# Two graph layers on listed neighbours: node rows two blocks ahead of the lists, and both weight folds moved to a later stage

## The chip, the cores and the metric

The kernel runs on one core of a Trainium2 chip. The metric is the device time of one execution in microseconds: 727.7 us, the median of three runs (726.72 to 728.53). One of these executions was also profiled; its span is 725.5 us, at a mean granted TensorE clock of 0.977. Engines are named as in the profile: PE is TensorE's matmul, PEld its weight load, DVE VectorE, ACT ScalarE, POOL GpSimd, SP the queue of SyncE.

## What is computed

`x` is 4096 x 512, `adj` a 4096 x 4096 matrix of int32 with about four ones in a row. Layer 0 is graph attention with eight heads, layer 1 a mean over neighbours with two linear maps and a third on their concatenation:

```python
# layer 0: W (8, 512, 64), a (8, 128)
Wh = einsum('nf,hfo->hno', x, W)
f1 = einsum('hno,ho->hn', Wh, a[:, :64]);  f2 = einsum('hno,ho->hn', Wh, a[:, 64:])
e  = leaky_relu(f1[:, :, None] + f2[:, None, :], 0.2)
attn = softmax(where(adj > 0, e, -9e15))
x  = layernorm(x + concat_heads(attn @ Wh))
# layer 1
deg = sum(adj > 0)
agg = (adj > 0) @ x / max(deg, 1)
y = concat(x @ W_self + b_self, agg @ W_nb + b_nb) @ W_comb + b_comb
x = layernorm(x + relu(y))
```

## The kernel before

The rows are taken in 32 blocks of 128. The adjacency is never used as a matrix: it is turned into a list of neighbours for each row, and the two layers gather their neighbours' rows by index. (A dense path, `dense_layers`, stands behind a flag and does not run on these inputs.) There are three stages, and each engine executes its own queue in the order of the program text (`manual_schedule`), so the text fixes what waits behind what.

**Lists and node rows (to about 245 us).** For each block `b`, `load_adj` brings two halves of 1 MB of `adj` into four buffers (`at`). `mask_adj` (ScalarE, L367) turns a half into bf16 (`ab`, three buffers) and so frees the list buffer. `fold_adj` (TensorE, L379) adds the eight segments of each row into one number per column, from which `decode` can read column and segment: a first matmul puts the column numbers into a PSUM bank (`cols`, weighted by `two`), two more add the weighted bits. `max_keys` (VectorE, L393) takes the largest eight of each quarter. Every four blocks, `decode` turns these keys into lists in five parts, one in each following iteration: keys apart; the top 16; degrees and the first three indices; the offsets of what is left over and the rows `sts` that assign it; and the "shared" slots (`es`, two a block) that take those neighbours beyond three. In the same iteration the node block's row is computed: `transposed` (L304, its copy L306), then `node_half` twice (L312), eight matmuls each, against `w_sb`, which holds W and, in eight columns on either side, W times the two halves of `a`. The result (`row`) is stored to `t0` in DRAM by ScalarE's queue.

Ahead of this stage stands a prologue: w0 is loaded, the extra columns of `w_sb` are computed in 32 operations of VectorE (L722, L727), and `fold_weights` computes `m2 = W_nb @ W_comb` (lower half) with its bias (L251 to L285). The list loads are issued behind the 2 MB of these weights.

**Attention (about 245 to 510 us).** `gather` (GpSimd, L508) fetches for each block three plus two rows of `t0` by index, five indirect transfers a block, into five buffers (GA). A loop over `i` from -2 to 33 runs the steps of different blocks against each other: `a_weights`, `a_exp`, `a_sum` for block i+2; `a_reach`, `a_normed`, `a_weigh`, `a_shared` (L595) for i+1; `a_moments` (L611), `root`, `norm` for i; and for i-1 `a_z` (L632), which multiplies the new row by `m2` and stores it to `t1`. In the first turns the last list parts and `m1 = W_self @ W_comb` (upper half) are worked in: `some(lists)`, `some([folds])`.

**Second layer (510 to 725 us).** Gathers from `t1`, five a block again; `g_self` (L656) with `m1`, `g_shared` (L663), adds, the norm, and the store. A gather buffer is free again when `g_shared` and the adds of the block five earlier are through.

PSUM has the banks `key` (1), `nm` (2), `pw` (2), `tp` (1) and `sm` (2). Small results go round in the two `sm` banks.

Of the kernel before, what the change touches and what calls it, by code (L numbers as in the profile page):

```python
# [22 lines left out]

# [16 lines left out]
P = 128  # L40
# [44 lines left out]
def listed_layers(  # L85
# [32 lines left out]
    EX = KX + 2 + 1 + H  # L118
# [67 lines left out]
    )  # L186
    two = const.tile([P, 32], BF16, name="two")
# [20 lines left out]
    es = const.tile([P, NB, KH, EX], F32, name="es")  # L208
    idx = const.tile([P, NB, KS], U32, name="idx")
# [4 lines left out]
    m1 = const.tile([P, FB, HD], F32, name="m1")  # L214
    brow = const.tile([P, HD], F32, name="brow")
    bc = const.tile([1, HD], F32, name="bc")
# [13 lines left out]
    def load_fold(k, w, fp):  # L230
        wr = fp.tile([P, FB, HD], F32, name="wr")
        (nc.sync, nc.scalar)[k].dma_start(wr, w.rearrange("(c p) o -> p c o", p=P))
        wc = fp.tile([P, FB, HD], F32, name="wc")
        (nc.sync, nc.scalar)[k].dma_start(
            wc, w_comb[k * HD : (k + 1) * HD, :].rearrange("(c p) o -> p c o", p=P)
        )
        return wr, wc
# [6 lines left out]
    def fold_weights(loaded, m, wp, tag="pw", last=None):  # L244

        wr, wc = loaded

        def turned(c):
            tp = ps.tile([P, FB, P], F32, name="nm", bufs=2)
            for d in range(FB):  # L250
                nc.tensor.transpose(tp[:, d, :], wr[:, c, ts(d, P)], ident)  # L251
            t = wp.tile([P, FB, P], F32, name="xT", bufs=2)
            nc.scalar.copy(t, tp)
            return t

        wT = turned(0)
        for c in range(FB):
            nxt = turned(c + 1) if c + 1 < FB else last and last()
            t = "pw" if c + 1 < FB else tag
            mp = ps.tile([P, HD], F32, name=t, bufs=2 if t == "pw" else 1)  # L260
            for d in range(FB):
                nc.tensor.matmul(  # L262
                    mp, lhsT=wT[:, d, :], rhs=wc[:, d, :], start=(d == 0), stop=(d == FB - 1)
                )
                if t != "pw" and d == FB // 2 - 1:
                    yield
            nc.scalar.copy(m[:, c, :], mp)
            wT = nxt
            yield

    def fold_bias(loaded, brw, to, tag):
# [5 lines left out]
        bp = ps.tile([1, HD], F32, name=tag, bufs=1)  # L277
        for d in range(FB):
# [4 lines left out]
            if d == FB // 2 - 1:  # L283
                yield
        nc.vector.tensor_add(brow[0:1, :], bp, to)  # L285
# [9 lines left out]
    def load_x(b, xacc):  # L295
        if b < NB:
            nc.sync.dma_start(xs[:, b, :], x[ts(b, P), :])
            nc.gpsimd.tensor_tensor(xacc, xacc, xs[:, b, :], OP.add)  # L298
# [19 lines left out]
    def node_rest(b, row):  # L318
# [3 lines left out]
        )  # L322

    def mean_row(w_sb, xacc, wp):
# [7 lines left out]
        nc.vector.tensor_copy(xm, pm)  # L332
        mr = wp.tile([P, HD], F32, name="y", bufs=2)
        mf = small.tile([1, H], F32, name="mf", bufs=1)
        for k in range(2):
# [9 lines left out]
            if k == 0:  # L345
                nc.vector.tensor_copy(mf, pq[:, 0:H])
        nc.scalar.dma_start(t0[1:2, 0:H], mf)
        nc.scalar.dma_start(t0[1:2, H:TW], mr[0:1, :])

# [3 lines left out]
    def load_adj(b, ap):  # L353

        if b < NB:
            for h in range(NH):
                at = loads[b, h] = ap.tile([P, NG // NH, SC], I32, name="at", bufs=4)
                r = b * P + h * (P // NH)
                nc.sync.dma_start(
                    at, adj[r : r + P // NH, :].rearrange("(j r) (s c) -> (r s) j c", r=RG, s=SEG)  # L360
                )

    def mask_adj(b, h, ap):
        if b == NB:
            return
# [5 lines left out]
    def fold_adj(b, dp):  # L371
# [3 lines left out]
        )  # L375
        ab = [masks.pop((b, h)) for h in range(NH)]
        for k in range(3):
            for t in range(P // 32):
# [4 lines left out]
                    start=(k == 0), stop=(k == 2), tile_position=(0, 32 * t),  # L383
                )
# [10 lines left out]
    def decode(b0, dp, wp):  # L395
# [48 lines left out]
        if b0 + G == NB:  # L444
            yield
        for b in range(b0, b0 + G):
            lt = wp.tile([P, KH * P], F32, name="st", bufs=2)
            nc.vector.tensor_scalar(lt, iota[:, 0 : KH * P], end[:, b : b + 1], None, OP.is_lt)
            if b0 + G < NB:
                st = wp.tile([P, KH * P], F32, name="own", bufs=4)  # L450
            else:
                if b % 2 == 0:
                    rows = wp.tile([P, FW], F32, name="row", bufs=2)
                st = rows[:, b % 2 * KH * P : (b % 2 + 1) * KH * P]
            nc.vector.scalar_tensor_tensor(
                st, iota[:, 0 : KH * P], lst[:, b, KL : KL + 1], lt, OP.is_ge, OP.mult
            )
            sts.append(st)
        yield
        pe = ps.tile([P, G, KH, EX], F32, name="sm", bufs=2)  # L460
# [6 lines left out]
        if b0 + G == NB:  # L467
            yield
        nc.vector.tensor_copy(es[:, bs], pe)
        if b0 + G == NB:  # L470
            yield
# [33 lines left out]
    def gather(table, b, gp):  # L505
        g = gp.tile([P, KS, TW], F32, name="g")
# [22 lines left out]
    def a_weights(b, wp):  # L529
        gw = G0[b][:, :, 0:H]  # L530
        e = E[b] = wp.tile([P, KS, H], F32, name="e", bufs=3)
        nc.vector.tensor_tensor(
            e[:, 0:K0, :], gw[:, 0:K0, :],
            lst[:, b, KL + 3 :].unsqueeze(1).to_broadcast([P, K0, H]), OP.add,
        )
        nc.vector.tensor_add(e[:, K0:KS, :], gw[:, K0:KS, :], es[:, b, :, KX + 3 :])
# [48 lines left out]
    def a_x(b):  # L585

        NM[b] = ps.tile([P, HD], F32, name="nm", bufs=2)
        if b < 2:
            nc.tensor.matmul(NM[b], lhsT=ident, rhs=xs[:, b, :], start=True, stop=False)
        else:  # L590
            nc.scalar.copy(NM[b], xs[:, b, :])

    def a_shared(b):
        for k in range(KH):
            nc.tensor.matmul(  # L595
                NM[b], lhsT=OWN[b][:, k, :], rhs=G0[b][:, K0 + k, H:TW],
                start=False, stop=(k == KH - 1), skip_group_check=b > 1,
# [88 lines left out]
    wp = ctx.enter_context(tc.tile_pool(name="work", bufs=1))  # L686
    dp = ctx.enter_context(tc.tile_pool(name="decode", bufs=1, side="right"))
    ap_cm = tc.tile_pool(name="lists", bufs=1, side="right")
    ap = ap_cm.__enter__()
    xa = ctx.enter_context(tc.tile_pool(name="xa", bufs=1))  # L690
    xacc = xa.tile([P, FIN], F32, name="xacc")
    nc.gpsimd.memset(xacc, 0.0)
    w_sb = xa.tile([P, FB, FW], F32, name="w_sb")
    with tc.tile_pool(name="wa", bufs=1) as wa:
        arow = wa.tile([1, H, 2, D], F32, name="arow")
        nc.scalar.dma_start(arow, a0.rearrange("h (k d) -> h k d", k=2).unsqueeze(0))
        for h in range(H):
            nc.sync.dma_start(
                w_sb[:, :, H + h * D : H + (h + 1) * D], w0[h].rearrange("(c p) o -> p c o", p=P)
            )  # L700
        loaded = load_fold(1, w_nb, wa)
        brw = load_bias(1)
        nc.scalar.dma_start(bc, b_comb.rearrange("(a o) -> a o", a=1))
        load_x(0, xacc)
        load_x(1, xacc)
        load_adj(0, ap)
        load_x(2, xacc)
        load_x(3, xacc)
        load_adj(1, ap)
        for b in range(4, XL):  # L710
            load_x(b, xacc)
        pads(wp)
        av = []
        for k in range(2):
            av.append(ps.tile([P, H, D], F32, name=("key", "sm")[k], bufs=(1, 2)[k]))
            nc.tensor.matmul(av[k], lhsT=oner, rhs=arow[:, :, 1 - k, :], start=True, stop=True)
        for a in range(2):
            for k in range(2):
                for c in range(FB):
                    pr = wa.tile([P, H // 2, D], F32, name="pr", bufs=2)  # L720
                    cs = slice(H + a * HH, H + (a + 1) * HH)
                    nc.vector.tensor_mul(  # L722
                        pr, w_sb[:, c, cs].rearrange("p (h d) -> p h d", d=D),
                        av[k][:, a * 4 : a * 4 + 4, :],
                    )
                    f = k * TW + a * 4
                    nc.vector.tensor_reduce(w_sb[:, c, f : f + 4], pr, AX.X, OP.add)  # L727
        last = {}

        def first():  # L730
            last["xT"] = transposed(0, wp)

        pieces = fold_weights(loaded, m2, wp, last=first)
        for c in range(FB):
            next(pieces)
            if 1 <= c <= 2:
                mask_adj(0, c - 1, ap)
        next(pieces, None)
        for _ in fold_bias(loaded, brw, bc, "key"):
            pass  # L740
    fp = ctx.enter_context(tc.tile_pool(name="fold", bufs=1))


    xT = last["xT"]
    row, lists = None, []
    for b in range(NB):
        load_x(b + XL, xacc)
        load_adj(b + 2, ap)
        if b == NB - 2:
            loaded = load_fold(0, w_self, fp)  # L750
            brw = load_bias(0)
        if b < NB - 1:
            for p in lists:
                next(p, None)
        mask_adj(b + 1, 0, ap)
        nxt = transposed(b + 1, wp) if b + 1 < NB else None
        if b > 0:
# [534 lines left out]
```

## Time and profile before

| stretch, us | what runs | transfers, GB/s | of note |
|---|---|---|---|
| 0 to 18.1 | loads, columns of `w_sb`, start of the fold | 278 | VectorE busy 10.06 us |
| 18.1 to 36.3 | fold of `m2`, first masks | 358 | TensorE busy 17.61 us |
| 36.3 to 54.4 | first blocks | 279 | |
| 72.5 to 229 | lists and node rows | 392 | VectorE 117.09 of 156.5 us |
| 245 to 290 | last list parts, fold of `m1`, first gathers | 196 | mean TensorE clock 0.85 |
| 290 to 500 | attention | 199 | TensorE 207.42, VectorE 192.81 of 210 us |
| 512 to 705 | second layer | 249 | GpSimd 145.87 of 193 us |

The table is read by stretches, since the stages have different limits and the shares of the whole span (PE 90%, DVE 68%, ACT 59%, POOL 48%) mix them. GpSimd's busy time counts 0.95 us of each gather; the next one starts 1.25 us after it, so a stretch with 78% is one in which GpSimd never rests. Some times that are used below: the masks of the last list start at 232.97 and 236.01; the first gather of attention starts at 246.14; the first `a_z` at 287.5, the second at 295.67; the first gather of the second layer at 509.78.

### The profile page before, as it was taken

What the parts mean: (1) busy time and instruction counts of PE and PEld (TensorE: products, weight loads), DVE (VectorE), ACT (ScalarE), POOL (GpSimd) and SP (SyncE); (2) the same over time, 40 slices, a digit from 0 to 9 for tenths busy, and PEclk for the clock granted to TensorE, in tenths of its full rate; (3) what the DMA queues carried; (4) which work ended last, traced back from release to release, by engine and by line L of the source; (5) the groups of instructions that cost most, each with busy time, mean ns of one, the idle gap of its engine ahead of it and who ended that gap; (6) DMA issues with size and microseconds to landing.
All of it is one profiled execution on the core that took longest, in us unless ns stands there. A gap on an engine that the chain in (4) does not pass through costs nothing.

```text
span 725.5 us, 9190 instructions
## 1 busy us (share of the span) xinstructions
PE 650.8 (90%) x2654; PEld 358.1 (49%) x2654; DVE 493.5 (68%) x1474; ACT 430.3 (59%) x883; POOL 348.5 (48%) x368
## 2 busy tenths in 40 slices
PE   4998888887899899999999999998999999999972
PEld 1465656655666654555555555554444444443320
DVE  5236777877877676899999999994255555554552
ACT  1566667666677123565766657665466666666653
POOL 3421122122100377566666666500677777777771
PEclk9999999999999889999999999999999999999995
DMA  9979999999999477677787887711588888878882
GB/s 278 358 279 394 393 393 392 392 393 392 392 393 389 163 211 211 185 230 230 226 234 225 230 230 229 227 41 39 173 257 250 252 252 255 251 249 249 250 256 101
DMA packets 84248, 191.29 MB, mean 264 GB/s; under 512 B 12496, under 2 KB 12504, under 8 KB 84190
## 3 DMA queue, kind: packets, MB, share of 16 engines
q0 software_dynamic: 25600, 84.56, 40.6%
q1 hardware_dynamic: 52896, 95.43, 35.7%
q10 hardware_dynamic: 5694, 10.64, 4.0%
q8 instruction: 23, 0.38, 0.2%
q14 instruction: 35, 0.29, 0.1%
HBM read 165.29 MB, written 25.31 MB: 263 GB/s over the span
## 4 chain that ended last, share of the span: by engine, by line
PE 50%; DMA 19%; POOL 10%; issue 9%; DVE 6%; ACT 5%; ACTq 0%; POOLq 0%; SPq 0%; DVEq 0%
PE pw L632 16%; POOL g L508 10%; DMA at<-in_adj_dram 9%; PE nm L595 8%; PE pw L312 7%; DMA g<-t,idx 6%; ACT xT L306 3%; PE pw L262 3%; PE tp L304 3%; DMA t<-row 2%; PE pw L663 2%; PE sm L546 2%; PE sm L463 1%; DMA w_sb<-in_L_gnn_W_dram 1%; PE nm L656 1%
## 5 line engine op out<-in xcount | busy, mean ns | idle before, releaser
L508 POOL DMA_INDIRECT g<-t,idx x320 | 303.3, 948 | 211.8 <-issue 120.2
L367 ACT ACTIVATE ab<-at 128x2048 bf16<-128x2048 int32 x64 | 122.2, 1910 | 62.9 <-DMA at<-in_adj_dram 56.1
L312 PE MATMUL pw<-w_sb,xT 128*128 128x264 f32 x512 | 127.6, 393 | 0.0
L632 PE MATMUL pw<-m,xT 128*128 128x512 f32 x256 | 118.4, 605 | 3.4 <-ACT xT L306 1.7
L298 POOL TENSOR_TENSOR xacc<-xacc,xs 128x512 f32<-128x512 f32 x32 | 41.3, 1292 | 148.7 <-DMA xs<-in_x_dram 148.2
L312 PEld LDWEIGHTS pw<-w_sb,xT 128*128 128x128 f32 x512 | 92.2, 190 | 26.1 <-issue 3.8
L306 ACT COPY xT<-tp 128x512 f32<-128x512 f32 x80 | 46.2, 578 | 72.1 <-PE tp L304 71.9
L580 DVE TENSOR_TENSOR g<-g,key 128x1024 f32<-128x1024 f32 x64 | 77.8, 1216 | 1.1
L632 PEld LDWEIGHTS pw<-m,xT 128*128 128x128 f32 x256 | 46.0, 189 | 56.8 <-issue 45.9
L304 PE MATMUL tp<-ident,xs 128*128 128x128 f32 x320 | 49.5, 277 | 26.3 <-ACT xT L306 25.3
L304 PEld LDWEIGHTS tp<-ident,xs 128*128 128x128 f32 x320 | 37.9, 141 | 61.0 <-ACT xT L306 32.2
L595 PE MATMUL nm<-g,own 128*128 128x512 f32 x128 | 62.7, 612 | 0.0
L656 PE MATMUL nm<-m,xT 128*128 128x512 f32 x128 | 57.7, 593 | 1.3 <-ACT xT L306 1.3
L656 PE MATMUL pw<-m,xT 128*128 128x512 f32 x128 | 57.6, 592 | 0.0
L316 DVE COPY row<-pw 128x264 f32<-128x264 f32 x64 | 27.3, 427 | 41.7 <-DMA t<-row 17.5
L642 ACT COPY sm<-g 128x512 f32<-128x512 f32 x32 | 18.9, 590 | 50.8 <-DMA g<-t,idx 47.8
L648 DVE TENSOR_TENSOR y<-sm,g 128x512 f32<-128x512 f32 x32 | 22.1, 691 | 30.8 <-DMA g<-t,idx 30.5
L663 PE MATMUL pw<-g,own 128*128 128x512 f32 x64 | 34.2, 651 | 9.0 <-DMA g<-t,idx 6.0
L663 PE MATMUL nm<-g,own 128*128 128x512 f32 x64 | 34.1, 641 | 8.4 <-DMA g<-t,idx 4.1
L656 PEld LDWEIGHTS nm<-m,xT 128*128 128x128 f32 x128 | 23.1, 190 | 24.5 <-issue 23.0
L646 DVE TENSOR_TENSOR sm<-sm,g 128x512 f32<-128x512 f32 x32 | 22.3, 697 | 18.6 <-DMA g<-t,idx 17.8
L670 DVE SCALAR_TENSOR_TENSOR sm<-y,lst,nm 128x512 f32<-128x512 f32 x16 | 12.1, 755 | 33.5 <-PE nm L663 33.5
(176 smaller groups left out, 1006.0 us busy)
## 6 DMA issues: line engine op xcount, KB each, us to landing
at<-in_adj_dram SPq DMA_DIRECT2D x64, 1024.0 KB, 10.8
t<-row ACTq DMA_DIRECT2D x32, 260.0 KB, 5.7
xs<-in_x_dram SPq DMA_DIRECT2D x32, 256.0 KB, 6.0
t<-row SPq DMA_DIRECT2D x32, 256.0 KB, 3.4
out_dram<-row SPq DMA_DIRECT2D x32, 256.0 KB, 3.7
g<-t,idx POOLq DMA_INDIRECT x320, 4.1
w_sb<-in_L_gnn_W_dram SPq DMA_DIRECT2D x8, 128.0 KB, 7.6
wr<-in_L_gnn_W_nb_dram ACTq DMA_DIRECT2D x1, 1024.0 KB, 7.2
```

The lines of the kernel that those rows point to most:

```text
L298: nc.gpsimd.tensor_tensor(xacc, xacc, xs[:, b, :], OP.add)
L304: nc.tensor.transpose(tp[:, c, :], xs[:, b, ts(c, P)], ident)
L306: nc.scalar.copy(t, tp)
L312: nc.tensor.matmul(pw, lhsT=xT[:, c, :], rhs=w_sb[:, c, k * HW : (k + 1) * HW], start=(c == 0), stop=(c == FB - 1),)
L316: nc.vector.tensor_copy(row[:, k * HW : (k + 1) * HW], pw)
L367: nc.scalar.activation(ab, loads.pop((b, h)), AF.Relu, accum_out=asum[:, b, h : h + 1])
L508: nc.gpsimd.indirect_dma_start(out=g[:, k, 0 : table.shape[1]], out_offset=None, in_=table[:, :], in_offset=bass.IndirectOffsetOnAxis(ap=i ...
L580: nc.vector.tensor_tensor(gv if to is None else to.rearrange("p (k h d) -> p k h d", k=1, h=H), gv, E[b][:, sl].unsqueeze(3).to_broadcast( ...
L595: nc.tensor.matmul(NM[b], lhsT=OWN[b][:, k, :], rhs=G0[b][:, K0 + k, H:TW], start=False, stop=(k == KH - 1), skip_group_check=b > 1,)
L632: nc.tensor.matmul(pz, lhsT=xT[:, c, :], rhs=m2[:, c, :], start=(c == 0), stop=(c == FB - 1))
L656: nc.tensor.matmul(NM[b], lhsT=xT[:, c, :], rhs=m1[:, c, :], start=False, stop=False, skip_group_check=True,)
L663: nc.tensor.matmul(NM[b], lhsT=OWN[b][:, k, :], rhs=g[:, K0 + k, 0:HD], start=False, stop=(k == KH - 1), skip_group_check=True,)
```

## The change

Several edits, meant to shorten the way to the first list load and to the first gather:

- **w0 first.** The prologue no longer loads or folds `w_nb`. w0, x's first block (on ScalarE's queue) and the lists come first. The extra columns of `w_sb` are computed in six operations of VectorE and two multiplications of GpSimd on tiles of 128 x 1024.
- **Node rows two blocks ahead.** The index `w` of the node block runs ahead of the list block `b`: in iterations 6 and 12 two node blocks are computed (`AHEAD`). So the loop over lists ends at block 29 with all rows in `t0`, and the lists 30 and 31 are folded while the first gathers run.
- **ScalarE writes the columns into the fold's bank.** `key_bank` copies the column numbers (`colf`) into the PSUM bank, and `fold_adj` leaves out its first matmul, save in blocks 0, 1 and 3, where each of the three banks is first used. The order of ScalarE in an iteration is now: `xT`, `key_bank`, store, both masks.
- **Last lists in the turn.** The parts of the last decode are spread over the first turns of attention (i = -2 to 0).
- **z's weights last.** `w_nb` and `w_comb` are loaded behind the last list, and `m2` is folded in chunks, one ahead of the attention loop and one in each of i = -2, -1, 0; its bias follows at i = 1. `m1` and its bias are folded between attention and the second layer. There is one buffer for `wT` where there were two.
- Small ones: `f1` of the neighbours' receivers is laid out once in `f1s` (GpSimd and VectorE), so `a_weights` needs one addition and not two; `a_x` is ScalarE's copy for all blocks.

```diff
     def decode(b0, dp, place):
...
+        nc.vector.tensor_copy(es[:, bs], pe[:, :, :, 0:EX])
+        nc.vector.tensor_copy(f1s[:, bs, K0:KS, :], pe[:, :, :, EX:])
...
+    def key_bank(b):
+        key = keys[b] = ps.tile([P, SC], F32, name=("key", "nm")[b % 2], bufs=(1, 2)[b % 2])
+        if b not in FIRST:
+            nc.scalar.copy(key, colf)
...
     def fold_adj(b, dp):
-        for k in range(3):
+        for k in range(0 if b in FIRST else 1, 3):
...
+    av = fp.tile([P, FB, HD], F32, name="wr")
+    nc.scalar.dma_start(av[0:1, 0:2]..., a0...)
+    for h in range(H):
+        nc.sync.dma_start(w_sb[:, :, H + h * D : H + (h + 1) * D], w0[h]...)
+    load_x(0, nc.scalar)
+    load_adj(0, ap)
+    load_x(1)
+    load_x(2)
+    load_adj(1, ap)
+    for b in range(3, XL):
+        load_x(b)
...
+    for a in range(2):
+        times(nc.gpsimd, a, pr1[a], av[:, 0])
+    times(nc.vector, 0, pr2, pa[1])
+    summed(0, 0, pr2)
+    times(nc.vector, 1, pr2, pa[1])
+    summed(1, 0, pr2)
+    summed(0, 1, pr1[0])
+    summed(1, 1, pr1[1])
...
+    for b in range(LB):
+        for k in range(1 + (b in AHEAD)):
+            load_x(w + k + XL)
+            sum_x(w + k + XL, xacc)
+        load_adj(b + 2, ap)
...
+        if b == LB - 1:
+            loaded = load_fold(1, w_nb, fp)
+        some(lists)
+        nxt = transposed(w + 1, wp) if w + 1 < NB else None
+        key_bank(b + 1)
+        if w > 0:
+            store(w - 1, row)
+        for h in range(NH):
+            mask_adj(b + 1, h, ap)
+        row = node_block(w, xT, b)
+        w, xT = w + 1, nxt
+        if b in AHEAD:
+            nxt = transposed(w + 1, wp)
+            store(w - 1, row)
+            row = node_block(w, xT)
+            w, xT = w + 1, nxt
...
+    mask_adj(NB - 1, 0, ap)
+    store(NB - 1, row)
...
+    for b in range(2):
+        G0[b] = gather(t0, b, gps)
+    m2s = chain(fold_weights(loaded, m2, fp, ("pw", "pw", "tp", "tp")), fold_bias(loaded, brw))
+    fold_adj(LB, dp)
+    max_keys(LB)
+    mask_adj(NB - 1, 1, ap)
+    key_bank(NB - 1)
     some(lists)
+    some(lists)
+    fold_adj(NB - 1, dp)
+    max_keys(NB - 1)
...
+    some(lists)
+    lists = [decode(NB - G, dp, on_rows)]
+    some(lists)
     a_owners(0, wp)
     a_owned(0, wp)
+    for k in range(3):
+        next(m2s)
     some(lists)
...
     for i in range(-2, NB + 2):
...
+        if i < 1:
+            for k in range(3):
+                next(m2s)
+        if i < 1:
             some(lists)
         if i == 1:
-            spread_bias()
+            for k in range(2):
+                next(m2s)
...
+            loaded = load_fold(0, w_self, fp)
+            brw = load_bias(0)
+    m1s = chain(fold_weights(loaded, m1, fp, ("key", "tp", "key", "tp")), fold_bias(loaded, brw))
+    for _ in m1s:
+        pass
+    spread_bias()
+    G1 = {b: gather(t1, b, gps) for b in range(GA - 1)}
```

## The prediction

> **What bounds the kernel now.** I read the forty-slice part of the page first, then stretches of busy time, then the chain of waits, then single engines in order of time. The kernel has three stages with different limits: lists and node rows up to 245 us, attention to 510, the second layer to 725.
>
> The stretches (columns: stretch, length, busy PE, PEld, DVE, ACT, POOL, clock, DMA share, GB/s) give the first limit:
>
> ```profile
> 0.00:40.00 40.00, 28.57 (x77) 13.13 (x77) 16.08 (x51) 12.69 (x19) 15.63 (x26) 1.00 0.97 319
> 40.00:46.00 6.00, 6.00 (x47) 3.83 (x45) 2.42 (x9) 4.36 (x5) 0.81 (x1) 1.00 0.35 119
> 46.00:229.00 183.00, 156.66 (x1010) 111.40 (x1007) 132.67 (x527) 123.12 (x138) 28.67 (x22) 1.00 1.05 391
> ```
>
> From 46 us on the transfers run at 391 GB/s and no engine is full: the adjacency stream is the limit. Before that it is starved. From 40 to 46 us it drops to 119 GB/s, because ScalarE's masks (L367), which free the list buffers, wait behind the weight fold of the prologue.
>
> In the attention stage the chain of waits (start, length, what) has a fixed rhythm:
>
> ```profile
> 400.32 3.70 PE pw L632 x8
> 404.02 0.34 PE sm L546 x4
> 404.37 1.82 PE nm L595 x4
> 406.19 0.45 PE tp L304 x4
> 406.64 0.02 issue
> 406.66 0.59 ACT xT L306
> 407.25 0.04 issue
> 407.30 3.70 PE pw L632 x8
> ```
>
> One block is 6.98 us: TensorE, plus the one copy it waits for. VectorE is on none of it. In the second layer GpSimd's gathers (L508) start every 1.25 us without a gap from 509.78 to the last at 708.81: 160 gathers, 200 us, and a tail of 15.7 us. There GpSimd's issue is the limit.
>
> At the seam between lists and attention two fold chunks of eight matmuls stand in TensorE's order of time:
>
> ```profile
> 249.66 4.97 PE L262 MATMUL pw<-wc,xT 128*128 128x512 f32 x8
> 255.12 3.60 PE L262 MATMUL pw<-wc,xT 128*128 128x512 f32 x8
> ```
>
> The same work takes 4.97 and 3.60 us; the mean clock in 247 to 249 us is 0.50. The slow one follows a wait.
>
> **What the Trainium skill says.** "TensorE: Matmul & The Clock Gate", What's actually happening: the array runs at half clock after about 3.4 us of idling, at full clock after about as much sustained work. The trace agrees on the halves (4.97 against 3.60); an idle time of 2.11 us ahead of 244.54 was already followed by slow matmuls. "DMA: Bandwidth & Descriptors", Issuing engines are not separate DMA queues: a load moved to another issuing engine saves only its issue time. So x's first block on ScalarE's queue counts as nothing here; no row isolates it. "GPSIMD Engine Reference", Elementwise: a two-input operation takes GpSimd about twice VectorE's time. Here 128x512 takes 1.29 us (L298) against 0.70 (L605).
>
> **Part 1, the stream: minus 9.9 us.** The stretch up to 54 us, summed in steps of 2 us, misses 4.8 MB against 393 GB/s, or 12.3 us. The start (first 4 us: 3 and 163 GB/s) costs 3.2 us and stays; the 256-byte pieces of w0 cost some 2 us and stay; 1.5 us of lesser dips I leave in as well. So 5.6 us come back, provided that the masks no longer wait. They shouldn't: the column sums become six VectorE operations and two GpSimd ones of 128x1024. VectorE's are about 1.15 us each (L580, 1024 elements, 1.22), GpSimd's twice 1.29 = 2.6 each, beside them. With w0 landed at about 8 us they end near 15, not 23.7, and the first list is folded at about 16 us, before buffers run out. Moving 2.1 MB of fold weights behind the last list saves 5.35 us. Two more t0 stores (0.53 MB) now precede the last list: plus 1.35. Sum: 5.6 + 5.35 - 1.35 = 9.6 us, with rounding of the landing times 9.9. The last list landed before at 232.4: transfers end at 239, and 2.1 MB of weights and 0.5 MB of stores (6.6 us) follow it. So it lands at 222.5.
>
> Hidden here: ScalarE's column copies (29 of 0.6 us) join 4.8 us of its work in 6.67 us per list, and spare TensorE four matmuls (0.4 us). A node block ahead costs TensorE 4.6 us twice, with 1.4 us spare per list; the lag of some 3 us is less than the 8 us of list data in flight. GpSimd's small f1 copies, the extra VectorE copy per four lists, a_weights with one operation less, and the block ahead's row stores stay beside the stream or beside TensorE: nothing.
>
> **Part 2, the turn from lists to attention: plus 6.2 us.** Call the last landing T. Before, z of block 0 started (L632) at 287.5 = T + 55.1 and of block 1 at 295.7 = T + 63.3; then 6.98 each. The gathers can start earlier now: the last row store is issued at T - 0.2 and takes 5.7 us under load, so T + 5.5 instead of 246.1 = T + 13.7. But TensorE's queue holds more behind them. I walk the queues with durations of before (fold chunk: transposes 0.45, copy 0.6, matmuls 3.5; shared product L595 1.82; list parts of VectorE 2.8, 3.3, 1.15, 3.9 and 2.0):
>
> - T + 2.8: the last list is folded; VectorE finishes the lists 24 to 27 at T + 7.8, part 1 of the last decode at 10.6, owners at 11.1.
> - 11.1 to 16.3: owners' transposes and fold chunk 0. The exponential of block 0 stands on ScalarE behind the chunk's copy: 17. Before, all folds but one were over when it ran.
> - 17.5 to 22.5: chunk 1. Then block 0's reach, weigh and shared product, 25 to 27; chunk 2 to 31.9.
> - The fourth part of the decode has its little matmul behind chunk 2, so VectorE stands until 32.1 and starts block 0's moments at 36.0. TensorE then waits for block 1's weights until 38.9.
> - Chunk 3, 41 to 46; the lists' product; transposes; z of block 0 at T + 48.8.
> - The bias (3.6 us of matmuls, a copy ahead, an add behind) now stands between z of block 0 and of block 1: z of block 1 at T + 60.6.
>
> This is with a warm array. TensorE waits over 2 us three times in it (before chunk 0, before block 0's shared product, 6 us before block 1's), and the half clock makes chunk 0, the products and part of chunks 2 and 3 longer: T + 73 if each such wait cools it and 4 us of work warm it. The same walk for before gives 291.6 warm and 297 cooled; it measured 295.7, three quarters of the way. I take T + 69.5, 6.2 later after the landing than before.
>
> The stage after it keeps 6.98 us a block.
>
> **Part 3, the seam to the second layer: plus 6.4 us.** The self fold was done by 285 us before, beside the lists. Now it stands in TensorE's queue after the last z, with one buffer for wT: four chunks of 0.45 + 0.6 + 3.7 and waits, 4.85 each, 19.4; bias transpose, copy and matmuls 4.5; add, spreading matmul, copy of brow, copy into the banks and xT 4.2, less the 2.4 that this start took before: g_self of block 0 starts 25.7 us later relative to the last z. GpSimd doesn't wait for it at first: 25 gathers (five buffers) keep it busy for 31.3 us, from 509.8 to 541.1. The 26th needs the first buffer, which block 0's product (L663) frees: it ended at 521.5, now at 547.2. GpSimd stands for 6.4 us. Afterwards TensorE needs 5.59 us a block (519.59 to 525.18) against 6.25 of gathers, so nothing more is lost, and nothing made up.
>
> **Sum.** -9.9 + 6.2 + 6.4 = +2.7: 730.4 us. Each part is several times larger than the sum, so the sign is weak.
>
> **Rivals.** *The turn runs warm* (T + 60.6, 2.7 us earlier after the landing than before): -9.9 - 2.7 + 6.4 = -6.2, so 721.5. For it: chunks fill waits, and the clock's window may not fall on them. Against: the rows of before show slow matmuls after 2.11 and even 1.17 us of waiting. *The turn runs cold*, or the stream still has a hole: T + 77 is 14 later, -9.9 + 14 + 6.4 = +10.5, 738. For it: three long waits; against: before was never that cold for long. *The seam is free* (the fold fits into the gathers' lead): -9.9 + 6.2 = -3.7, 724. Against it: TensorE was busy through this seam in before.
>
> **How the numbers follow.** Forecast 0.5, of which a third lies within 0.3% and two thirds above; warm turn or free seam 0.3; cold turn 0.2. Faster 0.3, same 0.17, slower 0.53. Range: 720 to 739, which leaves out about 2 in 10, beyond the warm and cold walks.
>
> **What would show it.** No dip near 40 us, and the last mask (L367) near 223 to 226 instead of 236, show part 1. The start of the first z against the last landing (T + 55 to 62), and a VectorE wait of about 4 us ahead of a list part, show part 2. One idle time of about 6 us of GpSimd after 25 gathers of the second layer shows part 3. Wrong I would be if the stream has new holes where two node blocks follow each other, if attention's block is no longer 6.98, or if GpSimd never stops in the second layer.

## The result, and the profile after

The changed kernel takes 734.8 us (median, 733.96 to 736.2) where the kernel before takes 728.0 on the same chip: a ratio of 1.0097, 95% interval 1.0075 to 1.012. It is slower by 7 us; the forecast was slower by 2.7 (730.4, range 720 to 739). The profiled execution has a span of 734.5 us against 725.5, so 9.0 us have to be found in the two traces. Four terms make them up:

| from the traces, us | before | after | difference | forecast |
|---|---|---|---|---|
| start of the last list's mask | 236.01 | 227.94 | -8.1 | -9.9 |
| from there to z of block 1 | 59.7 | 68.6 | +9.0 | +6.2 |
| GpSimd idle after 25 gathers of layer 2, beyond the usual spacing of 1.25 | 0 | 6.95 | +6.95 | +6.4 |
| last gather to the end | 16.7 | 17.9 | +1.2 | 0 |

The first two leave the first gather of layer 2 where it was: 510.69 against 509.78. Of the 9.0 us, 8.1 lie behind it.

**The stream.** The same stretches as before, of the changed kernel (stretch, length in us, busy time of PE, PEld, DVE, ACT, POOL, granted clock, DMA share, GB/s):

```profile
0.00:40.00 40.00, 23.92 (x105) 15.30 (x106) 16.37 (x44) 18.61 (x22) 21.82 (x31) 0.96 0.97 330
40.00:46.00 6.00, 5.46 (x34) 3.49 (x32) 0.92 (x5) 3.68 (x5) 1.42 (x2) 1.00 1.01 358
46.00:229.00 183.00, 158.88 (x895) 114.13 (x896) 138.44 (x565) 135.94 (x164) 31.98 (x50) 0.96 1.05 391
```

The hole is gone but for a remainder: 358 GB/s from 40 to 46 us instead of 119, with a dip to 299 from 44 to 46. And the list stage runs at 391 GB/s as before, with ScalarE's busy time up from 123.12 to 135.94 us, the column copies (15.4 us) included: the copies are beside the transfers. The last mask before and after, with what ended the wait ahead of it in brackets:

```profile
236.01 1.91 ACT L367 ACTIVATE ab<-at 128x2048 bf16<-128x2048 int32 x1 [0.58 <-PE key L379]
...
227.94 1.91 ACT L373 ACTIVATE ab<-at 128x2048 bf16<-128x2048 int32 x1 [0.99 <-DMA at<-in_adj_dram]
```

After the change the mask waits for its list, which landed at 227.56. Before, it waited for a bf16 buffer that TensorE's fold frees; the landing is not in that trace. The half-list was issued at 226.06, and the two before it landed 9.8 and 9.2 us after their issue, so an estimate for its landing is 235.3 to 235.9. By landings the gain is then about 8 us too.

**The turn.** TensorE's larger pieces in order of time (start, length, engine, line, operation, count; in brackets its idle time before it and what ended that). L264 is a fold chunk, L544 block sums that need an exponential, L590 the shared product, L627 z, L281 the bias fold:

```profile
239.69 0.69 PE L527 MATMUL sm<-ident,own 128*128 128x128 f32 x2 [4.63 <-DVE own L502]
...
241.91 6.15 PE L264 MATMUL pw<-wc,wT 128*128 128x512 f32 x8 [0.68 <-ACT wT L259]
...
250.70 3.70 PE L264 MATMUL pw<-wc,wT 128*128 128x512 f32 x8 [0.73 <-ACT wT L259]
...
257.57 3.42 PE L590 MATMUL nm<-g,own 128*128 128x512 f32 x4
...
273.23 1.02 PE L544 MATMUL sm<-e,own 128*128 128x8 f32 x4 [6.64 <-ACT e L538]
274.11 3.69 PE L590 MATMUL nm<-g,own 128*128 128x512 f32 x4
...
285.46 3.70 PE L627 MATMUL pw<-m,xT 128*128 128x512 f32 x8
...
289.36 1.96 PE L590 MATMUL nm<-g,own 128*128 128x512 f32 x4
...
291.73 3.59 PE L281 MATMUL sm<-wc,bcol 128*1 128x512 f32 x8 [0.25 <-ACT bcol L277]
```

After the wait of 4.63 us the first chunk takes 6.15 us and not 3.70; two shared products take 3.42 and 3.69 where the warm one takes 1.96. The granted clock is 0.50 from 242 to 246 us, in the first chunk, and from 272 to 276, in the second of the two products. VectorE stands behind the chunks twice, in its own order of time:

```profile
265.94 0.16 DVE L450 COPY lst<-sm 128x4 f32<-128x4 f32 x1 [5.25 <-PE sm L449]
...
284.35 0.29 DVE L472 COPY es<-sm 128x128 f32<-128x128 f32 x1 [7.31 <-PE sm L468]
```

From the last mask to z of block 1, before and then after (columns as above):

```profile
236.01:295.67 59.66, 54.50 (x203) 30.97 (x203) 42.85 (x146) 16.26 (x39) 35.39 (x37) 0.89 0.64 190
...
227.94:296.58 68.64, 48.99 (x168) 26.07 (x167) 38.23 (x126) 17.61 (x41) 36.69 (x39) 0.79 0.55 160
```

TensorE is busy for 5.5 us less in the longer turn, though at a lower clock, and idle for 19.7 us instead of 5.2. The turn got longer by waiting, not by more work on TensorE.

**The seam.** GpSimd's 25th gather of layer 2, the last that finds a buffer free, and the 26th, the first that has to wait for one (its wait ends with the buffer's release; the engine named in brackets is only the latest that the profile saw):

```profile
540.75 0.95 POOL L510 DMA_INDIRECT g<-t,idx  x1 [0.30 <-issue]
548.95 0.94 POOL L510 DMA_INDIRECT g<-t,idx  x1 [7.25 <-PE key L307]
```

TensorE shows what freed it: the self fold ends, g_self (L651) of block 0 starts at 535.04 and not at 508.31, and its shared product (L658), which releases the gather buffer, ends at 548.2.

```profile
535.04 3.70 PE L651 MATMUL nm<-m,xT 128*128 128x512 f32 x8 [1.31 <-ACT xT L309]
...
546.33 1.88 PE L658 MATMUL nm<-g,own 128*128 128x512 f32 x4
```

From there the gathers follow each other every 1.25 us to the last, so the 7 us are not made up.

### The profile page after: what moved, and what is told of

It reads as the page before. It is cut to its first block, busy times and chain, and to the rows that moved or that the text cites. A ratio compares the mean times of both kernels' runs of the same rounds, so it can differ in the third digit from the quotient of the medians.

```text
span 734.5 us, 9037 instructions
## 1 busy us (share of the span) xinstructions
PE 649.7 (88%) x2534; PEld 365.3 (50%) x2534; DVE 485.2 (66%) x1424; ACT 444.7 (61%) x915; POOL 358.4 (49%) x403
## 5 line engine op out<-in xcount | busy, mean ns | idle before, releaser
L315 PE MATMUL pw<-w_sb,xT 128*128 128x264 f32 x512 | 134.6, 409 | 2.7 <-DVE row L319 2.7
L627 PE MATMUL pw<-m,xT 128*128 128x512 f32 x256 | 118.4, 605 | 3.4 <-ACT xT L309 1.7
L315 PEld LDWEIGHTS pw<-w_sb,xT 128*128 128x128 f32 x512 | 96.6, 198 | 32.0 <-DVE row L319 5.6
L627 PEld LDWEIGHTS pw<-m,xT 128*128 128x128 f32 x256 | 46.0, 189 | 56.8 <-issue 45.9
L590 PE MATMUL nm<-g,own 128*128 128x512 f32 x128 | 65.9, 639 | 0.0
L307 PEld LDWEIGHTS tp<-ident,xs 128*128 128x128 f32 x320 | 40.1, 146 | 38.8 <-issue 32.1
L651 PE MATMUL nm<-m,xT 128*128 128x512 f32 x128 | 57.7, 593 | 1.3 <-ACT xT L309 1.3
L651 PE MATMUL pw<-m,xT 128*128 128x512 f32 x128 | 57.6, 592 | 0.0
L658 PE MATMUL nm<-g,own 128*128 128x512 f32 x64 | 31.9, 623 | 5.3 <-DMA g<-t,idx 5.3
L651 PEld LDWEIGHTS nm<-m,xT 128*128 128x128 f32 x128 | 23.1, 190 | 24.5 <-issue 23.0
L665 DVE SCALAR_TENSOR_TENSOR sm<-y,lst,pw 128x512 f32<-128x512 f32 x16 | 12.1, 755 | 35.0 <-PE pw L658 35.0
L651 PEld LDWEIGHTS pw<-m,xT 128*128 128x128 f32 x128 | 23.1, 190 | 23.4 <-issue 23.4
L658 PE MATMUL pw<-g,own 128*128 128x512 f32 x64 | 32.2, 625 | 1.3 <-DMA g<-t,idx 1.3
L544 PEld LDWEIGHTS sm<-e,own 128*128 128x128 f32 x128 | 19.6, 197 | 24.5 <-issue 13.4
```

The lines of the kernel that those rows point to most:

```text
L307: nc.tensor.transpose(tp[:, c, :], xs[:, b, ts(c, P)], ident)
L315: nc.tensor.matmul(pw, lhsT=xT[:, c, :], rhs=w_sb[:, c, k * HW : (k + 1) * HW], start=(c == 0), stop=(c == FB - 1),)
L590: nc.tensor.matmul(NM[b], lhsT=OWN[b][:, k, :], rhs=G0[b][:, K0 + k, H:TW], start=False, stop=(k == KH - 1), skip_group_check=True,)
L627: nc.tensor.matmul(pz, lhsT=xT[:, c, :], rhs=m2[:, c, :], start=(c == 0), stop=(c == FB - 1))
L651: nc.tensor.matmul(NM[b], lhsT=xT[:, c, :], rhs=m1[:, c, :], start=False, stop=False, skip_group_check=True,)
L658: nc.tensor.matmul(NM[b], lhsT=OWN[b][:, k, :], rhs=g[:, K0 + k, 0:HD], start=False, stop=(k == KH - 1), skip_group_check=True,)
```

## The experiments

They met different chips, which matters here: in the second group the kernel before took 727.1 us, in the first, third and fourth 797.6, 794.3 and 796.0. Times are therefore compared by ratios to before on the same chip, and starts within a group; the second group's chip is called the 727-us chip below. Line numbers move by one or two in some kernels.

**Group 1 (before 797.6 us).** The self fold left out, for layer 2 alone:

```diff
-            m1 = fp.tile([P, FB, HD], F32, name="m1")
             loaded = load_fold(0, w_self, fp)
+            m1 = loaded[0]
...
-    m1s = chain(fold_weights(loaded, m1, ...), fold_bias(loaded, brw))
+    m1s = fold_bias(loaded, brw)
```

> Left out: the fold of w_self with its half of w_comb between the layers; w_self as loaded serves as the matrix, the bias fold, its spread, the loads and everything of the second layer stay. Theory (the seam's fold holds up the second layer, and with it the five gather buffers): GpSimd's idle stretch of 7.25 us after the 25th gather of layer 2 shrinks to under 1 us, g_self of block 0 starts some 18 us earlier than 535.0, and the time falls by 6 to 7.5 us, to about 728. Rival (the end is set by something the fold does not hold up, such as the number of gathers or the three engines' work in each block): the idle stretch moves to later gathers and the time stays within 1.5 us of the changed kernel's 734.8.

The neighbour fold left out of the turn:

```diff
     def load_fold(k, w, fp):
-        wr = fp.tile([P, FB, HD], F32, name="wr")
+        wr = m2 if k else fp.tile([P, FB, HD], F32, name="wr")
...
-    m2s = chain(fold_weights(loaded, m2, ...), fold_bias(loaded, brw))
+    m2s = chain(range(3 * FB), fold_bias(loaded, brw))
```

> Left out: the fold of w_nb with its half of w_comb in the turn; w_nb is loaded straight into m2, so the transfers stay the same and the bias fold stays. Theory (four chunks of the fold on TensorE's queue stand ahead of the list steps and of blocks 0 to 2): z of block 1 starts at 279 to 284 instead of 296.6 and the time falls by 12 to 18 us, to 717 to 723. Rival (the list steps on VectorE and the gathers set the turn; TensorE's chunks lie beside them): z of block 1 moves by 3 us or less and the time stays over 731.

The list steps first in the turn:

```diff
         if i < 1:
-            for k in range(3):
-                next(m2s)
-        if i < 1:
             some(lists)
+        if i < 1:
+            for k in range(3):
+                next(m2s)
```

(and the same exchange ahead of the loop).

> One order changed, the whole computation kept: in the turn each step of the last four lists is issued ahead of the three pieces of the w_nb fold instead of behind them. VectorE waited 5.25 us for the triangle product and 7.31 us for the list product behind a chunk each. Theory (these waits are on the path to z of block 1): z of block 1 starts 4 to 8 us earlier than 296.6 and the time falls by 4 to 8 us, to 727 to 731. Rival (TensorE's own work from the last list to z of block 1 is the bound, and VectorE's waits lie beside it): under 1.5 us.

TensorE writes all columns:

```diff
-    FIRST = (0, 1, 3)
+    FIRST = tuple(range(NB))
```

> One part of the change undone: TensorE writes the column numbers of all blocks into the fold's bank again, ScalarE none. Theory (the stream of 32 MB is bound by its transfers, so both engines have room): the time stays within 1 us of the changed kernel's 734.8, and the last list's mask stays at 227.9 within 1 us. Rival (TensorE is close to a bound in the two-blocks-ahead steps or in the turn, where it folds the last lists): the time rises by 2 to 4 us; the opposite rival (ScalarE's queue was the close one): it falls by as much.

| kernel | ratio to before | interval | us | last mask | z of block 1 | GpSimd idle after 25 gathers |
|---|---|---|---|---|---|---|
| no self fold | 1.0002 | 0.9979 to 1.0025 | 800.5 | 228.32 | 310.41 | 0.0 |
| no neighbour fold | 1.0086 | 1.0055 to 1.0117 | 803.8 | 226.72 | 299.77 | 22.8 |
| lists first | 1.0257 | 1.0211 to 1.0303 | 816.0 | 227.74 | 310.32 | 21.0 |
| columns by TensorE | 1.0242 | 1.0207 to 1.0277 | 815.4 | 227.06 | 308.65 | 21.5 |

The absolute times of the expectations missed, because the chip is not the one they were written for. The changed kernel itself was not run on this chip, so the kernel with TensorE's columns, whose turn and seam are those of the change, stands in for it. Against it, leaving out the self fold gives 14.9 us and leaves no idle time after the 25th gather (it had 21.5; GpSimd now stops for 5.3 us ahead of the 31st), and leaving out the neighbour fold gives 11.6 us, with z of block 1 8.9 us earlier. Both folds are on the path on that chip. The lists-first order gives nothing there. For the columns only the trace decides: the last mask comes at 227.06 against 226.72 to 228.82 in runs of the changed lists stage, so in the stream it makes no difference who writes them; a difference in the turn was not measured.

Why is the seam's hole three times as long on that chip? The lists-first kernel there: TensorE's bias fold, the last gathers, and VectorE's addition that only needs the bias fold ("remote" marks a wait whose end the profile shows without an instruction that brought it about):

```profile
553.43 3.59 PE L281 MATMUL sm<-wc,bcol 128*1 128x512 f32 x8 [1.30 <-issue]
```

```profile
566.22 0.95 POOL L510 DMA_INDIRECT g<-t,idx  x1 [0.30 <-issue]
```

```profile
568.66 0.68 DVE L285 TENSOR_TENSOR brow<-sm,brow 1x512 f32<-1x512 f32 x1 [45.09 <-remote]
```

The product was done at 557.0; VectorE took it 11.6 us later, when the gathers had stopped for want of a buffer. In the first trace of the changed kernel the same addition came in the middle of the gathers, at 530.86, right behind its product.

**Group 2 (before 727.1 us).** The changed kernel again:

> The changed kernel itself, unedited, on the chip and beside the runs of before that the next three share. On a chip where before takes 728 us both theories expect 733 to 737 us. The first four experiments shared a chip on which before took 797.6 us; if this call meets it again, the theory that the seam and the turn cost more there (VectorE stood still from 557.0 to 568.7 beside the gathers of layer 2) expects a ratio of 1.02 to 1.03, and the rival, that the chip stretches all alike, 1.008 to 1.012.

735.1 us, ratio 1.0118 (1.0061 to 1.0175). Last mask 226.88, z of block 1 295.27 (68.4 us later), GpSimd idle 6.95: the figures of the first trace come back.

Six gather buffers, for which the self fold writes in place:

```diff
-    GA = 5
+    GA = 6
...
+    G0[2] = gather(t0, 2, gps)
...
-            m1 = fp.tile([P, FB, HD], F32, name="m1")
             loaded = load_fold(0, w_self, fp)
+            m1 = loaded[0]
```

> Six gather buffers instead of five, the whole computation kept; to make room the fold of w_self writes its chunks over w_self's own, in place. Theory (the seam's loss is that GpSimd runs out of buffers while the fold delays block 0): a sixth block's five gathers fill the 7 us that GpSimd stood idle after the 25th, and the time falls by 5 to 6.5 us against the changed kernel. Rival (from the seam on, layer 2 is bound by TensorE, ScalarE and VectorE's work in each block once its start is late, not by the gathers): the end stays where it was, within 1.5 us.

729.0 us, ratio 1.0023 (1.0009 to 1.0037): 6.1 us under the changed kernel of the same group (the profiled executions differ by 3.4). The gathers now run past the 25th, and GpSimd waits once, for the 31st:

```profile
545.86 0.95 POOL L510 DMA_INDIRECT g<-t,idx  x1 [0.30 <-issue]
550.85 0.94 POOL L510 DMA_INDIRECT g<-t,idx  x1 [4.04 <-issue]
```

Next to nothing was expected there, since six blocks of gathers last about as long as block 0 needs. In this trace g_self of block 0 ran slow, which cost 3 us, and so it did in the other kernel with six buffers, further below:

```profile
533.89 6.75 PE L651 MATMUL nm<-wr,xT 128*128 128x512 f32 x8 [1.30 <-ACT xT L309]
...
533.73 6.60 PE L652 MATMUL nm<-wr,xT 128*128 128x512 f32 x8 [1.30 <-ACT xT L310]
```

So the theory of the seam holds: the loss was the gathers' lead, short by one block, not layer 2's work in each block.

The late weights:

```diff
     def load_fold(k, w, fp):
+        q = (nc.sync, nc.scalar)[k]
...
-        nc.sync.dma_start(wc, ...)
+        q.dma_start(wc, ...)
...
-        if b == LB - 1:
-            loaded = load_fold(1, w_nb, fp)
...
     mask_adj(NB - 1, 1, ap)
+    loaded = load_fold(1, w_nb, fp)
```

> One place changed, the whole computation kept: w_nb and its half of w_comb are issued on ScalarE's queue after the last list's mask instead of on SyncE's right behind the last list's two loads. Theory (the two weights shared the transfers with the last lists, whose masks came 3.0 us apart there instead of 2.67): the last masks come 2.5 to 5 us earlier, about 223 to 225.5 instead of 227.9, the first fold chunk still finds its weights in time, and the time falls by 2 to 5 us. Rival (the lists land in the order of their issue and what follows them on the queue does not touch them): the masks stay, and the first chunk of the fold waits for its weights, so the time rises by 1 to 4 us.

735.3 us, ratio 1.0117 (1.008 to 1.0154), and the last mask did not move:

```profile
228.22 1.91 ACT L374 ACTIVATE ab<-at 128x2048 bf16<-128x2048 int32 x1 [0.91 <-DMA at<-in_adj_dram]
```

So the weights behind the last list didn't delay it; the theory falls. The transfers show why nothing was to be won: from 224 to 228 us they now carry only 136 GB/s, and the last list, issued at 218.14, still lands at 227.84. They also came in time, so the rival's loss didn't come either.

All three together:

> The whole computation kept; six gather buffers, the late weights and the list steps ahead of the fold pieces in the turn, together. If each theory holds and they add, the time is 11 to 18 us under the changed kernel's and under before by 4 to 11 us, 717 to 724 where before takes 728. If only the buffers hold, 728 to 730, which is no better than before.

730.6 us, ratio 1.0055 (1.0036 to 1.0073), above the six buffers alone. The order of the lists does what it was meant to do on VectorE, and loses it again. Its waits for the two list products:

```profile
260.29 0.17 DVE L451 COPY lst<-sm 128x4 f32<-128x4 f32 x1 [0.32 <-PE sm L450]
...
275.19 0.29 DVE L473 COPY es<-sm 128x128 f32<-128x128 f32 x1 [3.75 <-PE sm L469]
...
283.85 0.18 DVE L575 TENSOR_TENSOR key<-e,sm 128x16 f32<-128x16 f32 x1 [6.34 <-PE sm L564]
```

5.25 and 7.31 us became 0.32 and 3.75, but a new wait of 6.34 stands behind the last chunk, which now runs slow on TensorE:

```profile
276.75 5.38 PE L265 MATMUL tp<-wc,wT 128*128 128x512 f32 x8 [0.68 <-ACT wT L260]
```

z of block 1 comes 68.0 us after the last mask; 66.6 with six buffers alone, 68.4 in the changed kernel. Taking these two waits from VectorE did not shorten the turn.

**Group 3 (before 794.3 us).** Two pieces of the turn moved into TensorE's idle stretches, on six buffers:

```diff
     some(lists)
+    for k in range(3):
+        next(m2s)
     lists = [decode(NB - G, dp, on_rows)]
     some(lists)
     a_owners(0, wp)
     a_owned(0, wp)
-    for k in range(3):
-        next(m2s)
     some(lists)
...
+        if i == -1:
+            some([bias, bias])
         if i == 1:
-            for k in range(2):
-                next(m2s)
```

> The whole computation kept. On top of the six buffers, two pieces of the turn move into stretches in which TensorE stood idle: the first chunk of the w_nb fold goes ahead of the transposed owner marks (TensorE idle 4.7 us there), and its bias fold goes from between z of blocks 0 and 1 to behind the triangle product of the last lists (TensorE idle 6.4 us there). Theory (TensorE's queue, idle stretches included, sets the turn): z of block 1 starts 6 to 8 us earlier than 68.5 us after the start of the last list's mask, and the time falls by 6 to 8 us against the kernel with six buffers (729.0), to about 722, under before. Rival (VectorE's list steps or the gathers set the turn, so filled idle time only moves the waits, as it did when the list steps were put first): within 1.5 us of 729.

The neighbour fold left out, again, and the fold left out of the kernel before:

> Left out: the fold of w_nb in the turn, as in the second experiment (w_nb is loaded straight into m2, the bias fold stays), on five buffers, repeated since that one ran on the chip of 797.6 us. Theory (the fold's four chunks are most of what lengthened the turn from 60.1 to 68.6 us after the last list): z of block 1 starts 46 to 56 us after the start of the last list's mask and the time falls by 12 to 20 us, to 715 to 723. Rival (the list steps that were moved into the turn, and TensorE's granted clock of 0.5 there, set it without the fold too): z of block 1 starts at 62 us or later and the time falls by under 6 us.

```diff
-        pieces = fold_weights(loaded, m2, wp, last=first)
-        for c in range(FB):
-            next(pieces)
-            if 1 <= c <= 2:
-                mask_adj(0, c - 1, ap)
-        next(pieces, None)
+        first()
+        for h in range(NH):
+            mask_adj(0, h, ap)
```

> The kernel before, with the fold of w_nb in its opening left out (w_nb is loaded straight into m2; the loads of both weights and the bias fold stay), so that the first list's masks no longer wait behind the fold's copies on ScalarE. Theory (the fall of the transfers to 90 GB/s at 42 to 46 us was this wait, and the stream is bound by its transfers, so the whole hole comes back at the end): the fall vanishes and the time drops by 4.5 to 6 us, to about 722. Rival (the lists catch up before the stream ends, or the hole only moves): under 1.5 us.

**Group 4 (before 796.0 us)** was the ninth kernel once more:

> The whole computation kept; the ninth experiment's kernel again (six buffers, the first chunk of the w_nb fold ahead of the transposed owner marks, its bias fold behind the last lists' triangle product), since that run met a chip on which before took 794.3 us and hand-offs between engines stood still for 10 to 20 us beside the gathers. On a chip where before takes 727 us the theory (TensorE's queue with its idle stretches sets the turn) expects z of block 1 at 60 to 63 us after the start of the last list's mask (68.5 in the changed kernel, 66.6 with six buffers alone) and 721 to 724 us, a ratio of 0.992 to 0.996 to before; the rival (filled idle time only moves the waits) 66 to 68 us and 728 to 731 us. On a slow chip, where each expects about 1.023 as in the ninth, it decides nothing.

| kernel | ratio to before | interval | last mask | z of block 1 |
|---|---|---|---|---|
| chunk early | 1.0233 | 1.0192 to 1.0274 | 226.82 | 312.99 |
| chunk early, again | 1.0247 | 1.021 to 1.0284 | 227.21 | 314.41 |
| no neighbour fold | 0.9979 | 0.9951 to 1.0006 | 226.98 | 294.85 |
| before, no fold in the opening | 0.9941 | 0.9922 to 0.996 | 230.70 | 309.67 |

The kernel before without its opening's fold tests part 1. The hole is filled:

```profile
40.00:46.00 6.00, 5.74 (x37) 3.96 (x36) 1.99 (x8) 3.23 (x4) 0.05 (x1) 1.00 1.05 391
```

Its last mask starts 5.3 us earlier than 236.01 in the trace of before (that trace is of another chip; but the changed kernel's last mask starts at 226.7 to 228.8 on every chip, so the list stage can be compared), and the time falls by 3.8 us, 0.6%. The list stage keeps the gain; on this chip a part of it is lost later.

The early chunk decided nothing, twice. It did what was meant up to 242 us, with the exponential of block 0 at 242.44 and not at 248.58. Then ScalarE, which has nothing to do but take the second chunk's product from TensorE (done at 253.6), does so at 265.58, while gathers run back to back until 268:

```profile
265.58 0.59 ACT L269 COPY m<-pw 128x512 f32<-128x512 f32 x1 [18.26 <-remote]
272.65 0.37 ACT L529 COPY st<-sm 128x256 f32<-128x256 f32 x1 [6.48 <-remote]
```

In the kernel without the neighbour fold, VectorE rests about a microsecond between neighbouring instructions of its own in the same stretch:

```profile
265.26 0.35 DVE L461 TENSOR_SCALAR lt<-iota,end 128x256 f32<-128x256 f32 x1 [0.92 <-DVE row L462]
266.67 0.49 DVE L462 SCALAR_TENSOR_TENSOR row<-iota,lst,lt 128x256 f32<-128x256 f32 x1 [1.05 <-issue]
268.06 0.46 DVE L461 TENSOR_SCALAR lt<-iota,end 128x256 f32<-128x256 f32 x1 [0.91 <-issue]
```

So on these chips the turn is set by something else too. Even in the kernel before (without its opening's fold) z of block 1 comes 79.0 us after the last mask there, against 59.7 on the first chip. Without the fold z of block 1 still comes 67.9 us after the last mask, where 46 to 56 were expected (73.1 in the first group, where the same kernel had the ratio 1.0086 and not 0.9979: a ratio carries from one of these chips to another only to about 1%); with the early chunk it is 86.2, and the times differ by 19.7 us, though these two kernels also differ in buffers and order. None of this says how many microseconds the fold's chunks, or TensorE's idle stretches, are worth on the 727-us chip. That stays open: no kernel without the neighbour fold, and none with the early chunk, ran on it.

## Why the prediction was right, and where it was off

The direction and the signs of the three terms were right; the sum was 4 us short of the median, 6 short of the profiled execution. The misses of the three terms and the tail (1.8, 2.8, 0.6 and 1.2 us) all lie on the slow side. With a sum of +2.7, and a chance of 0.53 given to slower, that the sign came out right was in part luck.

- **Part 1, the hole.** "So 5.6 us come back": shown. Up to 54 us the stretches sum to 18.3 MB and not 16.4, which is 4.8 us at 393 GB/s (5.7 in the repeated run, 4.1 with the late weights), and leaving the fold out of the kernel before moved its last mask by 5.3.
- **Part 1, the landing.** "The last list landed before at 232.4" was wrong: it was taken from the end of the transfers minus all that was issued behind the list, as if loads landed one after another. The trace has 232.57 for the landing of the half before the last one; the last half is estimated above at 235.3 to 235.9, so the place was 3 us early. The forecast for after, 222.5, was early by 5: the list landed at 227.56, and the mask, named for 223 to 226, started at 227.94. The gain, -8.1 (-9.1 in the repeat), was close to -9.9 because both places were wrong alike, which is luck.
- **Part 1, hidden work.** The list stage held 391 GB/s through two blocks ahead and the column copies: shown by the trace, and in accord with the columns given back to TensorE.
- **Part 2, the turn.** "T + 69.5" for after was within 1 us: 68.6 and 68.4 after the last mask, 69.0 after the landing. Here the step that failed is the start for before: z of block 1 stood at T + 63.3 by the misplaced landing, at 59.7 by the mask (59.8 to 60.4 by the estimated landing). That is more than the whole difference between +6.2 and +9.0. The hit of 69.5 owes something to the same mistake: "three quarters of the way" from warm to cooled was read from a walk for before that, it seems, was counted from 232.4. Counted from 235.6 it gives 294.8 and 300.2, the measured 295.7 lies near the warm end, and the same rule would give about T + 63 for after (an estimate).
- **Part 2, the walk.** Its elements are in the trace: z of block 0 57.5 us after the mask (55 to 62 were named), VectorE's wait behind the chunk, 5.25 us (4 were named), the wait for block 1's exponential, 6.64 us (6), the bias between the two z. The halved clock takes 2.5 us in the first chunk and 1.5 and 1.7 in two shared products. But "TensorE's queue holds more behind them" is not what the traces show: its work in the turn fell from 54.5 to 49.0 us, and its waits grew from 5.2 to 19.7. The walk did have such waits (before chunk 0, before both shared products), the engines waiting for each other in turn. Which of them would have to go to shorten the turn was not shown: putting the lists first only moved VectorE's wait, and the test that was to fill TensorE's idle time gave no answer.
- **Part 3, the seam.** Predicted +6.4, measured 6.95 (the prediction's own times, 547.2 less 541.1, give 6.1; 6.4 counts in the usual pause of 0.3 us between two gathers). Shown from both sides: a sixth buffer gave 6.1 us, and without the fold the idle time behind the 25th gather vanished, on another chip. "25.7 us later relative to the last z": g_self follows the last z by 31.72 us, by 5.90 before, so 25.8. "25 gathers (five buffers) keep it busy for 31.3 us": shown.
- **Attention** keeps 6.98 us a block: shown.
- **The tail** was taken as unchanged. It is 1.2 us longer, of which 1.0 lies between the last gather's issue and the last shared product (4.08 against 3.08). After the change that product waited for its gather to land, before it waited for VectorE's additions; why the gather took longer is not known.
- **The clock.** "The trace agrees on the halves (4.97 against 3.60)": these two chunks are no halving, since only a part of the first ran at the low clock. The pair 6.75 and 3.70 comes near it.
- **Rivals.** The warm turn, T + 60.6, was wrong (68.6 to 69.0), the free seam was wrong (6.95 us of idle time). The cold turn, T + 77, was wrong on the 727-us chip (on the others, kernels with both folds had 81.6 to 87.2).

No version with the whole computation that was measured beat the kernel before: the nearest, six buffers, is at 1.0023.

## What to carry to other kernels

Work moved into a queue that feeds a pipeline costs what the pipeline's buffers can't bridge: before moving it, count the buffers' lead (25 gathers of 1.25 us here) against the delay of the first release. Here the lead was short by 7 us, a sixth buffer won back 6.1, and no new order that was tried won anything. A place on a loading queue is not a landing time; read a landing from issue and landing in the trace, and its consumer's start only where that consumer waited for it, in both kernels alike. When a stretch gets longer, compare an engine's work and its waits in it before calling the engine's queue the cause. And when an order is changed to take a wait from one engine, look for the place where it comes back (here 6.34 us behind the last chunk).

## What the runs showed of the hardware

- Three of the four chips of the experiments ran the kernel before 9 to 10% slower than 727.1 us. In the kernels traced there, hand-offs between engines stood still for 6 to 18 us while gathers were issued back to back, on VectorE as on ScalarE, though the transfers of the list stage kept 391 GB/s; and the change cost more there, 1.023 to 1.026 for its variants with the whole computation. All the lost time lies in stages with gathers. Set beside the kernel before on the first chip, the kernel without its opening's fold has a turn that is 19.3 us longer; attention from z of block 1 is longer by 10.3, the gathers of layer 2 by 28.6 and the tail by 12.0. In layer 2 GpSimd stops there for some 3 us, mostly after 15 gathers. The lines below show one such stop, and VectorE's wait that ends just before it does. The mechanism was not found.

```profile
678.00 0.76 DVE L670 SCALAR_TENSOR_TENSOR sm<-y,lst,pw 128x512 f32<-128x512 f32 x1 [11.16 <-remote]
...
678.70 0.95 POOL L508 DMA_INDIRECT g<-t,idx  x1 [3.37 <-ACT xT L306]
```

- The clock fell without any long wait. In the seam TensorE waited 0.77 and 1.30 us, with work between, in five traces alike, and these waits are shorter than the idle time of about 3.4 us in the prediction's citation. Then g_self took 3.70 us in the three traces with five buffers, 6.75 and 6.60 in the two with six. The Trainium skill, "TensorE: Matmul & The Clock Gate", What's actually happening, says that the activity window is free-running and that the same kernel varies with its phase; these traces are in accord with that but do not show it, since the split follows the number of buffers. Of the 14 executions with six buffers ten took 727.3 to 729.6 us and four, the profiled one among them, 731.1 to 732.0. So two traces of such a seam can differ by 3 us.
